# A selective-scan block with a feed-forward block: the input's row statistics formed one stage sooner

## The chip, the core and the metric

One core of one Trainium2 chip runs the kernel. The metric is device time in microseconds (us), the median over runs. The profile is of one execution on the same kind of core. Engines are called as in the profile: PE is TensorE (PEld its weight load), DVE is VectorE, ACT is ScalarE, POOL is GpSimd, and SP is SyncE, which issues every DMA of this kernel on one queue. The engines run side by side, and each works through its own instructions strictly in order.

## What is computed

The input `x` is 4 sequences of 2048 rows with 256 channels. A Mamba block and then a gated feed-forward block are added to it, each on rows that a layer norm has made ready:

```python
x = x + mamba(layernorm(x), ...)        # mamba adds its own input again
x = x + ffn(layernorm(x), ...)

# mamba
xn    = (x - mu) * rsqrt(var + 1e-5) * ln_w + ln_b
xi, z = split(xn @ W_in)                # 512 channels each
u     = silu(causal_conv4(xi) + conv_b)
dt_r, Bm, Cm = split(u @ W_xproj)       # 16, 64, 64
delta = softplus(dt_r @ W_dt + b_dt)
h_t   = h_(t-1) * exp(delta_t * A) + (delta_t * u_t) * B_t    # 512 channels x 64 states
y_t   = h_t . C_t
out   = x + ((y + u * D) * silu(z)) @ W_out
# ffn
out   = (silu(x @ wg.T) * (x @ wu.T)) @ wd.T                  # 768 hidden
```

The input of the Mamba block is a layer norm of a layer norm. The kernel forms both from one mean and one variance for each row.

## The kernel before

**Blocks and stages.** The 8192 rows are cut into 16 blocks of 512 rows (`NT` = 16, four for each sequence). The recurrence of a block is done in 16 groups of 16 pairs. A pair is a tile of 128 partitions (two channels times 64 states) by 512 time steps, and one `tensor_tensor_scan` on VectorE (line 1539) runs its whole recurrence. So a block needs 256 scans and the program 4096. A *stage* n, here and in the prediction, is the time of the 256 scans of block n. For each pair TensorE spreads delta over the states into a PSUM tile `a` (line 1528), ScalarE makes the decay factors with an exp in place (line 1534), and VectorE scans. There are four `a` tiles, so ScalarE can be at most four scans ahead. The other factor, delta times u times B, comes from a broadcast load of `dusc` into a tile `ring` (three of them, each one group) and is multiplied on GpSimd (line 1645). After its scan, TensorE contracts the ring with C (line 1563).

**Dense work.** While the scans of block n run, the other engines prepare block n+1 and finish block n-1. The function at line 1628, `dense`, takes these parts in order:

- `front(n+1)`: load x (`load_x`), row statistics (`layer_norm`), normalise into `xn`, store the residual to `rsum`, transpose to `xnT`
- `back(n-1)`: gate y, project out, add the residual, form sums for the second norm
- `front_a(n+1)`: project `xi` and convolve into `u`
- `front_b(n+1)`: project z (`project_z`), one silu over `u` and both z tiles (lines 997 to 1001: a table load, three activations, and a table load back to exp), then the dt projection, B and C, and four rounds of softplus
- `back_b(n-1)`: the feed-forward block, with a silu of its own (lines 1264 to 1267)

**How `layer_norm` works.** For the input (`sums` is None) VectorE runs four `bn_stats` on 128 x 256 each (line 491), then four `bn_aggr` (line 492) that write mean and variance into a PSUM bank `lp`. ScalarE then does five small steps on that (two of line 530, then 540, 541, 542: variance plus eps, log, exp, square), and VectorE does three small ones (545, 550, 555), one step of Newton's method and the bias. The results are two small tiles `rs` and `nm`.

**The planner.** The order of instructions on each engine isn't written by hand. Every operation is noted with an engine, a reckoned cost, what it reads and writes, and, for dense work, a due step. `dense` spreads due steps evenly over the stage by cumulated cost, from scan 8 to scan 244 (`D_SPAN`):

```python
tot = sum(o.cost for o in os)
t, lo, hi = 0.0, n * 256 + span[0], n * 256 + span[1]
for o in os:
    o.step = lo + (hi - lo) * t / tot if n >= 0 else -1000
    t += o.cost
```

`Planner.run` then places operations one by one. For each engine it takes the ready operation with the lowest score, which is its earliest start plus a bias. Work of the scan stream (kind S) has bias 0; dense work (kind D) has 17 ns for each step that it is ahead of its due step, kept between -230 and 170. So dense work that is late goes ahead of a scan that is ready at the same time, and dense work that is early goes behind it. ScalarE and TensorE add 300 ns to an operation that would hold up the stream. `after=` makes an operation ready when another one *starts*, without a data dependence.

**Buffers.** Named tiles rotate. `w4` has four (128 x 1024 floats); it carries `xt`, `xn`, `xnT`, the two z tiles `szs` (the gate buffers), and x1, xn, xT, hmb of `back_b`. Turns are taken strictly in program order, so a load into a `w4` tile can be issued only when all the turns before it have been taken and one tile is free. `ps` has four PSUM banks. Dense work takes banks in program order too, and only when two of them are free. `s4` has eight small tiles, `bst` four.

Of the kernel before, what the change touches and what calls it, by code (L numbers as in the profile page):

```python
# [20 lines left out]
P = 128  # L21
T = 512
DM = 256
DI = 512
# [314 lines left out]
def mamba_ffn_kernel(  # L339
# [5 lines left out]
    nc = tc.nc  # L345
# [30 lines left out]
    op, buf = pl.op, pl.buf  # L376
# [14 lines left out]
    win = const("win", [P, 2, 2 * DI])  # L391
# [38 lines left out]
    def tok(t):  # L430
        return t.t.rearrange("p a t -> p (a t)").rearrange("p (s c) -> p s c", s=4)
# [32 lines left out]
            one(s)  # L464
        return sums

    def layer_norm(src, blocks=range(4), twice=False, sums=None):

        nb = len(blocks)
        m = 2 if twice else 1
        lp = buf("ps")
        sq4 = buf("s4") if sums else None
        ve, rs, nm = buf("s4"), buf("s4"), buf("s4")

        def sq():
            return lp.t[:, 16 : 16 + m * nb]

        def col(b):  # L480
            return b.t[:, 0 : m * nb]

        def mv():
            return lp.t[:, 0 : 2 * nb].rearrange("p (s c) -> p s c", c=2)

        def two(v):
            return v.rearrange("p (m s) -> p m s", m=m)

        def stats(j, s):
            st = buf("bst")  # L490
            op("DVE", 326, lambda: nc.vector.bn_stats(st.t, tok(src)[:, s, :]), [(src, s // 2)], [st])
            op("DVE", 205, lambda: nc.vector.bn_aggr(mv()[:, j, :], st.t), [st], [(lp, 0, j)])

        def spread(s):
            op(
                "ACT", act(DM, ptr=1) + ACC,
                lambda: nc.scalar.activation(
                    lp.t[:, DM : 2 * DM], tok(src)[:, s, :], AF.Square,
                    bias=sums.t[:, 4 + s : 5 + s], accum_out=sq4.t[:, s : s + 1],
                ),  # L500
                [(src, s // 2), (sums, 4)], [(lp, 2), (sq4, s)],
            )

        if sums is None:
            for j, s in enumerate(blocks):
                stats(j, s)
            mk = [(lp, 0, j) for j in range(nb)]
        else:
            op(
                "ACT", 180,  # L510
                lambda: nc.scalar.activation(sums.t[:, 4:8], sums.t[:, 0:4], AF.Copy, scale=-1.0 / DM),
                [(sums, s) for s in range(4)], [(sums, 4)],
            )
            op(
                "ACT", 180, lambda: nc.scalar.copy(lp.t[:, 0:4], sums.t[:, 4:8]), [(sums, 4)], [(lp, 3)],
            )
            for s in range(4):
                spread(s)
            mk = [(sq4, s) for s in range(4)]

        def var_in():
            return mv()[:, :, 1] if sums is None else sq4.t[:, 0:4]

        def minus_mean():
            return mv()[:, None, :, 0] if sums is None else lp.t[:, None, 0:4]

        def var(i):
            op(
                "ACT", 180,
                lambda: nc.scalar.activation(  # L530
                    ve.t[:, i * nb : (i + 1) * nb], var_in(), AF.Copy,
                    bias=EPS * EPS if i else EPS, scale=(1.0 + EPS if i else 1.0) / (1 if sums is None else DM),
                ),
                mk, [(ve, i)],
            )

        for i in range(m):
            var(i)
        vk = [(ve, i) for i in range(m)]
        op("ACT", 180, lambda: nc.scalar.activation(col(rs), col(ve), AF.Ln), vk, [rs])  # L540
        op("ACT", 180, lambda: nc.scalar.activation(col(rs), col(rs), AF.Exp, scale=-0.5), [rs], [rs])
        op("ACT", 180, lambda: nc.scalar.activation(sq(), col(rs), AF.Square), [rs], [(lp, 1)])
        op(
            "DVE", TINY,
            lambda: nc.vector.scalar_tensor_tensor(sq(), sq(), -0.5, col(ve), ALU.mult, ALU.mult),
            [(lp, 1)] + vk, [(lp, 1)],
        )
        op(
            "DVE", TINY,
            lambda: nc.vector.scalar_tensor_tensor(col(rs), sq(), 1.5, col(rs), ALU.add, ALU.mult),  # L550
            [(lp, 1), rs], [rs],
        )
        op(
            "DVE", TINY,
            lambda: nc.vector.scalar_tensor_tensor(  # L555
                two(nm.t[:, 0 : m * nb]), minus_mean().to_broadcast([P, m, nb]), 1.0 if sums else -1.0,
                two(rs.t[:, 0 : m * nb]), ALU.mult, ALU.mult,
            ),
            (mk if sums is None else [(lp, 3)]) + [rs], [nm],
        )  # L560
        return rs, nm
# [197 lines left out]
    rest, gates, norms, last = {}, {}, {}, {}  # L759
# [12 lines left out]
    def front(n):  # L772
        r = n % R
        xt = load_x(n) if n else x0
        rs, nm = layer_norm(xt, twice=True)
        rp = buf("s4")
        op("ACT", 180, lambda: nc.scalar.activation(rp.t[:, 0:4], rs.t[:, 0:4], AF.Copy, bias=1.0), [rs], [rp])
        xn = buf("w4")
        normalise(xn, xt, (rs, nm), o=4)

        def keep():
            normalise(xt, xt, (rp, nm))
            store(rsum[r], lambda: tok(xt), 524288, halves(xt), [("rsum", r)])

        if n:
            keep()
        else:
            last["keep"] = keep
        xnT = buf("w4")

        def ev_t(c):
            def ev(ps):
                op(
                    "ACT", act(T, True, 2),
                    lambda: nc.scalar.activation(  # L795
                        xnT.t[:, c, :], ps.t, AF.Identity, bias=lnb[:, c : c + 1], scale=lnw[:, c : c + 1]
                    ),
                    [ps, "lnw", "lnb"], [(xnT, c)],
                )

            return ev

        for c in range(2):
            transposes(xn, c, ev_t(c))
        rest[n] = xnT
# [66 lines left out]
    def project_z(n):  # L872
        xnT = rest[n][0]
        szs = gates[n] = [buf("w4"), buf("w4")]

        def ev_z(k):
            def ev(ps):
                op(
                    "ACT", act(T, True), lambda: nc.scalar.copy(szs[k // 2].t[:, k % 2, :], ps.t),
                    [ps], [(szs[k // 2], k % 2)],  # L880
                )

            return ev

        for k in range(4):
            project(win, DI + k * P, xnT, ev_z(k), ["win"])

    def mix(n):
        r = n % R
# [98 lines left out]
    def front_b(n):  # L988
        b, q, r = n // NQ, n % NQ, n % R
        xnT, u = rest[n]  # L990
        uk = [(u, k) for k in range(4)]
        if n:
            project_z(n)
            szs = gates[n]
            zk = [(z, k) for z in szs for k in range(2)]

            def silu():
                nc.scalar.activation(u.t, u.t, AF.Silu)
                for h in range(2):
                    nc.scalar.activation(szs[h].t, szs[h].t, AF.Silu)  # L1000
                nc.scalar.preload_act_table_set(EXP_LN)

            o = op("ACT", 6400, silu, uk + zk, uk + zk)
            o.tail = -1283.0
            for k in uk:
                o.tails[k] = -3250.0
        else:

            def silu_a():
                nc.scalar.activation(u.t[:, 0:3, :], u.t[:, 0:3, :], AF.Silu)  # L1010

            def silu_b():
                nc.scalar.activation(u.t[:, 3, :], u.t[:, 3, :], AF.Silu)
                nc.scalar.preload_act_table_set(EXP_LN)

            op("ACT", 2900, silu_a, uk[0:3], uk[0:3])
            op("ACT", 1900, silu_b, uk[3:4], uk[3:4]).tail = -1283.0

        dtr = buf("xi")

        def mm_dt(k):
            return (
                430,
                lambda ps: nc.tensor.matmul(
                    ps[32 * k : 32 * k + 32, :], framed(wxp, k), u.t[:, k, :], start=True, stop=True
                ),
            )

        def ev_dt(ps):
            op(  # L1030
                "ACT", act(T, True, 1),
                lambda: nc.scalar.activation(dtr.t[:, 0:T], ps.t, AF.Identity, bias=dm[:, 2:3]), [ps, "dm"], [dtr],
            )

        last["dt"] = job([mm_dt(k) for k in range(4)], uk + ["wxp"], ev_dt)[-1:]

        rest[n] = (xnT, u, dtr)
        for m in range(2 if n == 0 else 0):
            softplus(n, m)
        mix(n)  # L1040
        for m in range(4 if n else 0):
            softplus(n, m)
        if n:
            gate(n)
# [673 lines left out]
```

## Time and profile before

| | |
|---|---|
| median of 3 runs | 4940.54 us (4936.31 to 4943.96) |
| profiled execution | 4944.55 us, of which the span of instructions is 4942.8 |
| granted TensorE clock | 0.976 |
| DMA | 1299.87 MB, mean 263 GB/s, 68.6% of the 16 engines' time in the queue of SP |
| `bn_stats` (L491) | 68 times, 409 ns median |
| `bn_aggr` (L492) | 68 times, 166 ns median |
| load of x (`w<-in`, 512 KB) | 15 times, 8.6 us median from issue to landing |
| reload of x1 (`w<-rsum`, 512 KB) | 31 times, 8.3 us median |
| silu of u and z (L998 to L1001) | 15 times, 6.4 us |
| stages 1 to 14, first scan to first scan | 299.5 to 307.5 us |

A line of the groups names source line, engine, operation, what it writes and reads, tile shapes and count; after the bar stand busy time in us and the mean of one in ns, then idle time of the engine just before these instructions and who ended it. A line of the timeline has start, length, engine, line, operation and count; a number in brackets is idle time of the engine before it.

### The profile page before, as it was taken

What the parts mean: (1) busy time and instruction counts of PE and PEld (TensorE: products, weight loads), DVE (VectorE), ACT (ScalarE), POOL (GpSimd) and SP (SyncE); (2) the same over time, 40 slices, a digit from 0 to 9 for tenths busy, and PEclk for the clock granted to TensorE, in tenths of its full rate; (3) what the DMA queues carried; (4) which work ended last, traced back from release to release, by engine and by line L of the source; (5) the groups of instructions that cost most, each with busy time, mean ns of one, the idle gap of its engine ahead of it and who ended that gap; (6) DMA issues with size and microseconds to landing.
All of it is one profiled execution on the core that took longest, in us unless ns stands there. A gap on an engine that the chain in (4) does not pass through costs nothing. (4 is left out here: it accounts for less than half of the span.)

```text
span 4942.8 us, 116006 instructions
## 1 busy us (share of the span) xinstructions
PE 4433.3 (90%) x46924; PEld 2205.2 (45%) x46924; DVE 4734.0 (96%) x4576; ACT 4005.2 (81%) x7378; POOL 4695.2 (95%) x862
## 2 busy tenths in 40 slices
PE   7889989998988999989999899989989999898888
PEld 3434444444444444444444444444444444444435
DVE  7999999999999999999999999999999999999996
ACT  6788878778788887888878788887878878888774
POOL 6999999999999999999999999999998999999994
PEclk9999999999999999999999999999999999999999
DMA  8676776667766777677667676677776767676762
GB/s 295 237 282 252 284 272 266 265 242 287 265 266 257 272 266 280 263 266 279 262 264 278 259 277 255 263 291 267 274 263 247 280 265 282 255 290 253 264 248 86
DMA packets 306347, 1299.87 MB, mean 263 GB/s; under 512 B 33617, under 2 KB 134737, under 8 KB 174866
## 3 DMA queue, kind: packets, MB, share of 16 engines
q1 hardware_dynamic: 305810, 1292.44, 68.6%
q8 instruction: 369, 6.05, 0.5%
q14 instruction: 168, 1.38, 0.1%
HBM read 1186.94 MB, written 105.38 MB: 261 GB/s over the span
## 5 line engine op out<-in xcount | busy, mean ns | idle before, releaser
L1539 DVE TENSOR_TENSOR_SCAN ring<-a,ring 128x512 f32<-128x512 f32 x4096 | 4594.2, 1198 | 103.7 <-ACT a L1534 81.2
L1645 POOL TENSOR_TENSOR ring<-ring,b 128x4088 f32<-128x4088 f32 (+2 forms) x512 | 4540.0, 8897 | 154.3 <-DMA ring<-dusc 116.9
L1534 ACT ACTIVATE a<-a,a 128x512 f32<-128x512 f32 x4096 | 2702.2, 666 | 677.2 <-PE a L1528 647.1
L1528 PE MATMUL a<-stk,selb 128*128 128x512 bf16 x5088 | 1809.3, 391 | 407.4 <-DVE ring L1539 374.7
L1563 PE MATMUL ps<-ring,cz 128*32 128x128 f32 x32768 | 1235.9, 280 | 19.4 <-issue 12.4
L1528 PEld LDWEIGHTS <-selb 128*128 128x128 bf16 x5088 | 471.2, 98 | 1347.6 <-issue 1274.2
L1563 PEld LDWEIGHTS ps<-ring,cz 128*32 128x32 f32 x32768 | 811.1, 110 | 541.4 <-issue 478.0
L596 PE MATMUL ps<-w,wgu 128*128 128x512 f32 x720 | 373.5, 600 | 0.0
L1584 ACT COPY mm<-ps 128x512 f32<-128x512 f32 x512 | 304.5, 596 | 37.2 <-PE ps L1563 36.3
L1597 PE MATMUL ps<-mm,exs 128*32 128x128 f32 (+1 forms) x4112 | 285.3, 407 | 1.3 <-ACT mm L1584 1.0
L596 PE MATMUL ps<-w,win 128*128 128x512 f32 x512 | 260.7, 594 | 0.3 <-ACT w L795 0.3
L830 PE MATMUL ps<-xi,w 128*128 128x512 f32 x480 | 245.8, 593 | 0.0
L1597 PEld LDWEIGHTS ps<-mm,exs 128*32 128x32 f32 x4112 | 116.8, 118 | 202.8 <-ACT a L1534 81.6
L1148 PE MATMUL ps<-wd,w 128*128 128x256 f32 x720 | 195.8, 386 | 0.0
L596 PEld LDWEIGHTS ps<-w,wgu 128*128 128x128 f32 x720 | 138.1, 192 | 111.2 <-issue 58.5
L1148 PEld LDWEIGHTS ps<-wd,w 128*128 128x128 f32 x720 | 132.4, 189 | 42.1 <-issue 14.7
L949 PE MATMUL ps<-w,ident 128*128 128x512 f32 x248 | 133.3, 620 | 6.7 <-ACT ps L944 5.9
L596 PEld LDWEIGHTS ps<-w,win 128*128 128x128 f32 x512 | 96.8, 190 | 89.7 <-issue 57.5
L1148 PE MATMUL ps<-wout,w 128*128 128x256 f32 x480 | 128.4, 388 | 0.9
L830 PEld LDWEIGHTS ps<-xi,w 128*128 128x128 f32 x480 | 88.9, 188 | 82.6 <-issue 62.2
L571 ACT ACTIVATE w<-w,s,s 128x256 f32<-128x256 f32 x192 | 112.8, 597 | 0.9 <-DVE s L555 0.9
L1255 POOL TENSOR_TENSOR w<-w,w 128x512 f32<-128x512 f32 x90 | 113.4, 1281 | 0.0
(154 smaller groups left out, 2416.9 us busy)
## 6 DMA issues: line engine op xcount, KB each, us to landing
ring<-dusc SPq DMA_DIRECT2D x1023, 1024.0 KB, 7.9
stk<-dsc SPq DMA_DIRECT2D x256, 96.0 KB, 5.9
qd<-w SPq DMA_DIRECT2D x32, 512.0 KB, 9.5
szd<-w SPq DMA_DIRECT2D x32, 512.0 KB, 11.6
dusc<-w SPq DMA_DIRECT2D x63, 256.0 KB, 6.4
dsc<-pk SPq DMA_DIRECT2D x63, 256.0 KB, 6.5
rsum<-w SPq DMA_DIRECT2D x31, 512.0 KB, 6.8
w<-rsum SPq DMA_DIRECT2D x31, 512.0 KB, 8.3
```

Of the source, the lines that this page charges most:

```text
L596: lambda ps: nc.tensor.matmul(ps, w[:, c, o : o + P], xT.t[:, c, :], start=(c == 0), stop=(c == 1)),
L830: lambda: nc.tensor.matmul(ps.t, dg.t[:, j * P : (j + 1) * P], xi.t[:, j : j + T], start=(j == 0), stop=(j == 3)),
L949: lambda: nc.tensor.matmul(ps.t, m, t.t, start=False, stop=True, skip_group_check=True),
L1148: lambda ps: nc.tensor.matmul(ps[:, (s % 2) * DM : (s % 2 + 1) * DM], src(k)[:, s * P : (s + 1) * P], w[:, k, :], start=False, stop=(k == ...
L1255: "POOL", 1230, lambda: nc.gpsimd.tensor_tensor(hm(k), hm(k), up.t, ALU.mult),
L1528: "PE", 216, lambda: nc.tensor.matmul(a.t, selb[:, p, :], stk.t, start=True, stop=True),
L1534: lambda: nc.scalar.activation(a.t, a.t, AF.Exp, scale=a2f[:, idx : idx + 1]), [a, "a2"], [a],
L1539: nc.vector.tensor_tensor_scan(v, a.t, v, 0.0, ALU.mult, ALU.add)
L1563: nc.tensor.matmul(pm.t[cg * 32 : cg * 32 + 32, (r8 % 4) * P : (r8 % 4 + 1) * P], framed(cz, blk), ring.t[:, :, blk * 8 : blk * 8 + 8], st ...
L1584: nc.scalar.copy(mm.t[:, hb * 4 : hb * 4 + 4].rearrange("p r a t -> p (r a t)"), pm.t)
L1597: nc.tensor.matmul(ex.t[jh * 32 : jh * 32 + 32, a * 16 : b * 16], framed(exs, jh * 2 + jl), mm.t[:, a:b, :, jh * 2 + jl], start=(jl == 0), ...
L1645: e.tensor_tensor(v, v, b2.t[:, None, t0:].to_broadcast([P, m, T - t0]), ALU.mult)
```

## The change

After the last z projection of block m, `front_b(m)` now also loads the x of block m+1 and runs its whole `layer_norm`, and keeps `rs` and `nm` in `norms`. The `bn_stats` carry `after=`: they may start once the last z matmul has started. `front(m+1)`, a stage later, loads x once more and takes the kept statistics; if there are none (block 0 and block 1) it forms them as before. So the statistics of blocks 2 to 15 move, and 14 loads of 512 KB are added. In program order the new `w4` turn lies between the gate buffers and the x1 of `back_b`, and the new `ps` turn between the last bank of z and the bank of the dt projection.

```diff
-    def layer_norm(src, blocks=range(4), twice=False, sums=None):
+    def layer_norm(src, blocks=range(4), twice=False, sums=None, after=()):
...
         def stats(j, s):
             st = buf("bst")
-            op("DVE", 326, lambda: nc.vector.bn_stats(st.t, tok(src)[:, s, :]), [(src, s // 2)], [st])
+            op("DVE", 326, lambda: nc.vector.bn_stats(st.t, tok(src)[:, s, :]), [(src, s // 2)], [st], after=after)
             op("DVE", 205, lambda: nc.vector.bn_aggr(mv()[:, j, :], st.t), [st], [(lp, 0, j)])
...
     def front(n):
         r = n % R
         xt = load_x(n) if n else x0
-        rs, nm = layer_norm(xt, twice=True)
+        rs, nm = norms.pop(("in", n), None) or layer_norm(xt, twice=True)
...
         for k in range(4):
-            project(win, DI + k * P, xnT, ev_z(k), ["win"])
+            last["z"] = project(win, DI + k * P, xnT, ev_z(k), ["win"])[-1]
...
         if n:
             project_z(n)
+            if n + 1 < NT:
+                xt = load_x(n + 1)
+                norms["in", n + 1] = layer_norm(xt, twice=True, after=[last["z"]])
             szs = gates[n]
```

## The prediction

> **What bounds the kernel now.** First the busy table and the groups. VectorE is busy 4734.0 us of a 4942.8 us span, most of it in 4096 scans:
>
> ```profile
> PE 4433.3 (90%) x46924; PEld 2205.2 (45%) x46924; DVE 4734.0 (96%) x4576; ACT 4005.2 (81%) x7378; POOL 4695.2 (95%) x862
> ...
> L1539 DVE TENSOR_TENSOR_SCAN ring<-a,ring 128x512 f32<-128x512 f32 x4096 | 4594.2, 1198 | 103.7 <-ACT a L1534 81.2
> ```
>
> The scans are the clock of the program. Back to back, one starts 1.115 us after the other (median of 3777 neighbours; 1198 ns is the record, whose ends overlap). So only VectorE's idle time, 209 us, and its other work can be won. The view of waits says what the scans lack:
>
> ```profile
> DVE ring L1539 <- ACT a L1534: 81.2, 43, 4.9
> ```
>
> 43 times they wait for the exp on ScalarE, 4.9 us at the longest. The timeline of VectorE, then ScalarE, around the silu of u and z in stage 7 shows one of these:
>
> ```profile
> 2304.97 6.77 DVE L1539 TENSOR_TENSOR_SCAN ring<-a,ring 128x512 f32<-128x512 f32 x6
> 2315.98 4.57 DVE L1539 TENSOR_TENSOR_SCAN ring<-a,ring 128x512 f32<-128x512 f32 x4 [4.24 <-ACT a L1534]
> ```
> ```profile
> 2308.87 1.28 ACT L998 ACT_TABLE_LOAD   x1
> 2310.16 1.91 ACT L998 ACTIVATE w<-w 128x2048 f32<-128x2048 f32 x1
> 2311.98 1.99 ACT L1000 ACTIVATE w<-w 128x1024 f32<-128x1024 f32 x2
> 2313.99 1.28 ACT L1001 ACT_TABLE_LOAD   x1
> 2315.28 2.40 ACT L1534 ACTIVATE a<-a,a 128x512 f32<-128x512 f32 x4
> ```
>
> ScalarE is away for 6.4 us; the four `a` buffers carry the scans 2.9 us into it, then VectorE idles 4.24 us. This hole (4.0 to 4.9 us in stages 1 to 14, 2.8 in stage 0) is the one the change aims at. But there is a second one, at the silu of the feed-forward part. Stage 6, VectorE:
>
> ```profile
> 2109.28 5.65 DVE L1539 TENSOR_TENSOR_SCAN ring<-a,ring 128x512 f32<-128x512 f32 x5
> 2114.85 0.47 DVE L1458 TENSOR_TENSOR ps<-ps,a 128x128 f32<-128x128 f32 x2
> 2115.23 1.39 DVE L491 BATCH_NORM_STATS2 bst<-w 128x6 f32<-128x256 f32 x4
> 2116.57 0.07 DVE L820 MEMSET xi<- 128x3 f32 x2
> 2117.78 4.57 DVE L1539 TENSOR_TENSOR_SCAN ring<-a,ring 128x512 f32<-128x512 f32 x4 [1.14 <-ACT a L1534]
> ```
>
> The statistics of the next block's input already lie in it, at all 13 feed-forward silus that have a next block. Only the aggregates and the last three small steps stand between scans, at the start of a stage:
>
> ```profile
> 2194.72 0.16 DVE L492 BATCH_NORM_AGGREGATE ps<-bst 128x2 f32<-128x6 f32 x1
> 2194.79 1.19 DVE L1539 TENSOR_TENSOR_SCAN ring<-a,ring 128x512 f32<-128x512 f32 x1
> 2195.89 0.16 DVE L492 BATCH_NORM_AGGREGATE ps<-bst 128x2 f32<-128x6 f32 x1
> 2195.97 1.19 DVE L1539 TENSOR_TENSOR_SCAN ring<-a,ring 128x512 f32<-128x512 f32 x1
> 2197.07 0.39 DVE L492 BATCH_NORM_AGGREGATE ps<-bst 128x2 f32<-128x6 f32 x2
> 2197.37 2.32 DVE L1539 TENSOR_TENSOR_SCAN ring<-a,ring 128x512 f32<-128x512 f32 x2
> 2199.61 0.15 DVE L545 SCALAR_TENSOR_TENSOR ps<-ps,s 128x8 f32<-128x8 f32 x1
> 2199.66 1.21 DVE L1539 TENSOR_TENSOR_SCAN ring<-a,ring 128x512 f32<-128x512 f32 x1
> ```
>
> **The change, part by part.** It moves the statistics of blocks 2 to 15 (14 moves) and adds 14 loads of 512 KB.
>
> 1. The four `bn_stats` (1.33 us by their starts) leave the feed-forward hole. That hole's end is set by ScalarE's table load and exp, so nothing is won: its idle time grows from some 1.4 to 2.7 us. In their new place they use 1.33 of 4.24 us: also nothing. If that cover is missed they cost 1.33 x 13 = 17.3 us.
>
> 2. Aggregates and small steps leave a full stretch. Scan starts 1.18 us apart with one aggregate between them, against 1.115, price it: 0.066 us each for two, 0.288 for the pair (median of 14), 0.056, 0.0715 and 0.0705 for L545, L550, L555; together 0.62 us. Won if all hide: 14 x 0.62 = 8.7 us. Their records alone say 4 x 0.171 + 0.155 + 2 x 0.14 = 1.12 us, or 15.7 us, the far end of the gain; I take 0.62, since the scans' starts are what counts.
> The Trainium skill (VectorE: DVE Perf Modes, the section on the TRN2 errata) holds that every small operation pays a fixed term, measured at about 150 cycles of 0.96 GHz. As an estimate from that page, seven such terms are 1.09 us, and 14 blocks would give 15.3 us in place of 8.7; the scans' starts above speak against it.
>
> 3. The small ScalarE steps (two L530, L540, L541, L542) take 0.87 us at the start of stage 7 (2197.49 to 2198.36 us). Now they come due as the silu ends, where VectorE waits for the first exp. Ahead of it they lengthen the hole by 0.87; behind it they cost nothing: 0 to 14 x 0.87 = 12.2 us. I take half, 6.1.
>
> 4. Place in VectorE's queue. The planner prefers an operation that is past its due step. Adding the kernel's own costs, 78,534 of 205,815 precede the new load in a stage, so it is due at step 8 + 236 x 0.38 = 98; the silus come at scan 109 to 116 of their stage. So the statistics are late and pass any scan that is ready, once their data and the last z matmul (some 2 to 3 us before the silu) allow. In 5 of the 13 stages the second gate buffer is taken 11 us before the silu, so x is there early and the statistics (2.1 us) push the last scans into the silu. These fill only what the four buffers hold, so between 0 and one scan of 1.115 us is lost. I take 0.5: 2.5 us.
>
> 5. In the other 8 stages the gate buffer is taken 3.3 to 3.5 us before the silu, and x can only be issued then. The nearest row is `w<-rsum`, also 512 KB, issued at that very place (it takes the next turn of the same buffers): in the six stages with a record it landed 2.0 to 5.6 us after the silu's start. Statistics then end at 4.1 to 7.7, the next scan wants VectorE at 7.1: loss 0 to 0.6, I take 0.2 x 8 = 1.6 us. The slowest ring load there took 13.95 us: issued 2.9 before the silu it would land at 11.1, and cost 6 us. Behind the waiting `bn_stats` stand all later scans.
>
> 6. DMA and queues. 512 KB at the mean 263 GB/s is 2.0 us, after 0.6 us of issue on SP, ahead of ring loads. GpSimd waits for these 116.9 us in all, but its products are ready 7 to 12 us before their scans in this part of a stage: nothing. Without that lead, 14 x 2 = 28 us. The reload of x1 in `back_b`, one turn later, slips by some 2 us; its first reader comes 11 us after the silu's start.
>
> 7. The aggregates hold a PSUM bank through the silu, and the dt projection takes its bank after them, so it may start 3 to 5 us later. The stores that hang on it go out up to scan 159 (first half) and are read from scan 237 on: nothing; the cover is some 75 scans. The next stage's normalisation, whose statistics now exist, starts a few us sooner; it is not on the path either.
>
> Sum: -8.7 + 6.1 + 2.5 + 1.6 = +1.5 us on the profiled execution's 4944.55, so 4946. That execution lies 4.0 above the median of 4940.54: **4942 us**, no change that counts. A measurement of this kernel tells about 0.2% (10 us) from no change. Around this stands the re-planning of the whole order: the stages 1 to 14 take 299.5 to 307.5 us from first scan to first scan for nearly equal work, so a shift of 1 us in each, 14 us in all, is easy either way. That makes the forecast's own range 4930 to 4954.
>
> **Rivals.**
> - *Faster, 4925:* everything hides behind the exps and frees its whole record, 15.7 us, or the new order loses less elsewhere. For it: the hole has 4.24 us for 2.1 us of work. Against: scan starts show 0.62, and the costliest part was hidden before.
> - *Slower by queue order, 4960:* point 4 holds in every stage. The statistics go ahead of the scans before the silu, a whole scan is lost to the four buffers, and the ScalarE chain stands ahead of the exps: 14 x (1.115 + 0.87) - 8.7 = +19. It decides once more than some 9 of 14 silus do so. For it: the due steps. Against: 8 stages get x too late for that.
> - *Slower by a late x, 4965:* `bn_stats` placed on an arrival that comes 2 us late in each: 14 x 2 - 8.7 + 6.1 = +25. For it: two of the 13 waited for `w<-in` already, 0.13 and 0.56 us, with 5.3 us of lead. Against: the `w<-rsum` landings.
>
> **How the numbers follow.** Forecast 0.42, faster 0.22, queue order 0.26, late x 0.10. So faster 0.22, same 0.42, slower 0.36. The likeliest case gives 4942; the range, 4921 to 4970, takes in the three rivals.
>
> **What would show it.** Right: `bn_stats` near L998, that hole at 2 to 3 us, the feed-forward hole grown to 2.5 to 3, no aggregates at a stage's start, stage lengths unmoved. Queue order: `bn_stats` with starts before L998's table load, and L530 between L1001 and the first exp. Late x: waits of L491 for `w<-in` of over 1 us. The forecast is wrong if stages change by more than 0.7 us each, wherever that comes from.

## The result, and the profile after

The changed kernel takes 5017.07 us, median of 4 runs (5006.78 to 5024.72), against 4938.43 us of the kernel before, timed beside it (4 runs, 4931.7 to 4943.96). The ratio is 1.0155 with a 95% interval of 1.0142 to 1.0168: 78.6 us slower (78 us in what follows), and outside the predicted range. The profiled execution has a span of 5014.4 us at a granted clock of 0.969 (before 4942.8 us at 0.976), 71.6 us more.

The busy table, the group of the scans and two waits of the changed kernel (in a wait: engine, tile and line that waited, who ended it, sum in us, times, longest; lines behind the edit stand three lower down, so 1542 is the scan, 1537 its exp and 1648 GpSimd's product):

```profile
PE 4405.9 (88%) x46629; PEld 2224.0 (44%) x46920; DVE 4736.4 (94%) x4576; ACT 4006.8 (80%) x7378; POOL 4696.0 (94%) x862
...
L1542 DVE TENSOR_TENSOR_SCAN ring<-a,ring 128x512 f32<-128x512 f32 x4096 | 4597.7, 1199 | 158.4 <-ACT a L1537 126.8
```
```profile
DVE ring L1542 <- ACT a L1537: 126.8, 78, 6.6
...
ACT w L942 <- DMA dusc<-w: 82.1, 21, 7.1
```

VectorE is busy for as long as before (4736.4 against 4734.0 us). What grew is its idle time. The scans waited 43 times for an exp, 81.2 us in all; now 78 times, 126.8 us. And ScalarE, which makes the exps, waits in line 942 for a *store*, `dusc<-w`, 82.1 us in all. The same line stood in the view of waits before:

```profile
ACT w L942 <- DMA dusc<-w: 15.4, 11, 3.6
```

Sorting VectorE's idle time over 50 ns by where it stands, from both traces, gives where the 71.6 us went (2.4 of them are busy time, 69 idle time):

| idle time of VectorE, us | before | after |
|---|---|---|
| at the silu of u and z | 62.8 | 42.6 |
| at the silu of the feed-forward part | 23.3 | 40.5 |
| scans waiting for an exp elsewhere | 16.3 | 79.1 |
| scans elsewhere, waiting for nothing that the profile shows | 1.5 | 19.6 |
| scans elsewhere, waiting for GpSimd | 0.3 | 3.3 |
| other instructions of VectorE elsewhere | 99.6 | 87.7 |

The first row is the gain that the change can aim at (after it, 26.8 of the 42.6 us stand ahead of a moved small step, line 545, and not ahead of a scan), and the second is the price of it that step 1 gives. The third, 62.8 us more, is what the prediction has no term for. Of the 102 us in rows three to five after the change, 90.3 stand in, or less than 12 us behind, a wait of ScalarE for one of two stores, `dusc<-w` (line 942) or `dsc<-pk` (line 956); before, 8.5 of 18.1 did.

One such place, in stage 9, where the scans stand still for 6.64 us. The timeline of the changed kernel, VectorE first, then ScalarE, then SP:

```profile
2990.22 0.66 DVE L957 TENSOR_TENSOR w<-ps,w 128x512 f32<-128x512 f32 x1
2990.80 4.55 DVE L1542 TENSOR_TENSOR_SCAN ring<-a,ring 128x512 f32<-128x512 f32 x4
3002.00 2.34 DVE L1542 TENSOR_TENSOR_SCAN ring<-a,ring 128x512 f32<-128x512 f32 x2 [6.64 <-ACT a L1537]
```
```profile
2992.38 0.28 ACT L962 COPY x<-w 128x64 f32<-128x64 f32 x1
2992.51 0.70 ACT L1537 ACTIVATE a<-a,a 128x512 f32<-128x512 f32 x1
2993.09 0.63 ACT L974 CAST pk<-ps 128x512 bf16<-128x512 f32 x1
3000.78 0.63 ACT L942 ACTIVATE w<-w 128x512 f32<-128x512 f32 x1 [7.06 <-DMA dusc<-w]
3001.32 0.64 ACT L1537 ACTIVATE a<-a,a 128x512 f32<-128x512 f32 x1
```
```profile
2984.28 2.53 SPq L425 DMA_DIRECT2D ring<-dusc  x4
2990.91 0.33 SPq L428 DMA_DIRECT2D dusc<-w  x1
```

A round of softplus makes delta times u in a tile `w` (line 957) and stores it to `dusc`. The next round takes a `w2` tile for a temporary (`rl`, line 942), and it is the very tile that the store is still reading. Line 942 stands in ScalarE's order, so the exps behind it wait too: the four `a` tiles carry the scans for another 2 us or so, then VectorE stands. The store lands 9.8 us after its issue, at 3000.7 us. Four ring loads of 1 MB each went out on the same queue between 2984.28 and 2986.81 us, ahead of the store; the last of them landed at 3000.05 us. The windows of the changed kernel show them (length in us, busy time and count of PE, PEld, DVE, ACT, POOL, then the granted clock, the DMA engines' share and GB/s):

```profile
2986.00:2988.00 2.00, 2.00 (x14) 0.75 (x15) 2.00 (x3) 1.80 (x5) 2.00 (x1) 1.00 0.90 381
...
2996.00:2998.00 2.00, 0.00 (x0) 0.00 (x0) 0.00 (x0) 0.00 (x0) 2.00 (x1) 1.00 0.97 348
2998.00:3000.00 2.00, 0.00 (x0) 0.00 (x0) 0.00 (x0) 0.00 (x0) 2.00 (x1) 0.76 0.32 116
```

The DMA engines are full (0.90 to 1.05 in all windows from 2986 on) up to 2998 us, and the store lands when they have run empty. In the last two windows everything but GpSimd stands still for it.
The Trainium skill (DMA: Bandwidth & Descriptors, the section on queues, rings and completion order) says that each DMA engine consumes its descriptors in ring order. A store issued after 4 MB of loads on one queue is then moved after them, and these windows agree.

**Why that tile.** The planner gives a tile back when the operation that was *placed last* among its users ends. The store is placed first; after it comes the copy of line 962, a short operation of ScalarE that saves the block's first column and reads the same tile. In the plan this store ends at 171.53 us of its stage, the copy earlier, and line 942 is put into the tile at 167.48. Counted in the plan, a tile is taken ahead of the end of its store at 11 places before the change (seven of them by under 1 us) and at 25 after it (six of them by these 4.05 us, at most by 4.6 us). The places where line 942 waits longest in the trace are among them. The generated program still waits for the landing, so nothing is overwritten; the wait is only one that the plan doesn't know of. Its own total went *down* with the change, from 4892 to 4885 us.

### The profile page after: what moved, and what is told of

Its sections match the earlier page's. It is cut to its first block, busy times and chain, and to the rows that moved or that the text cites. A ratio compares the mean times of both kernels' runs of the same rounds, so it can differ in the third digit from the quotient of the medians.

```text
span 5014.4 us, 115723 instructions
## 1 busy us (share of the span) xinstructions
PE 4405.9 (88%) x46629; PEld 2224.0 (44%) x46920; DVE 4736.4 (94%) x4576; ACT 4006.8 (80%) x7378; POOL 4696.0 (94%) x862
## 5 line engine op out<-in xcount | busy, mean ns | idle before, releaser
L1542 DVE TENSOR_TENSOR_SCAN ring<-a,ring 128x512 f32<-128x512 f32 x4096 | 4597.7, 1199 | 158.4 <-ACT a L1537 126.8
L1531 PE MATMUL a<-stk,selb 128*128 128x512 bf16 x4806 | 1755.5, 394 | 417.5 <-DVE ring L1542 381.8
```

Of the source, the lines that this page charges most:

```text
L1531: "PE", 216, lambda: nc.tensor.matmul(a.t, selb[:, p, :], stk.t, start=True, stop=True),
L1542: nc.vector.tensor_tensor_scan(v, a.t, v, 0.0, ALU.mult, ALU.add)
```

## The experiments

**Theory A:** the 78 us are these waits for stores, in one particular order of instructions; moving the statistics isn't what costs. **Rival B:** the statistics ahead of the scans at the silu, with ScalarE's small chain ahead of the exps, cost it. **Rival C:** the second load of x, or any new order of that length, costs it. A kernel's ratio is to the kernel before, run beside it, whose median was 4936 to 4942 us throughout.

**1. The same order with more tiles.** Each of the four `w2` tiles becomes two that alternate. The planner still counts four, so every engine's order of instructions is that of the changed kernel, and a round that takes a tile finds in it the one that was left a turn earlier. To make room, the up projection of the feed-forward part uses the gate's weights, and two of the six slices of the down projection's weights are used twice. Instructions and transfers are the same in number and size, but the result is not that of the block: a kernel to measure with, not to use.

```diff
-        "w2": tiles("w2", 4, [P, T]),
+        "w2": tiles("w2", 8, [P, T]),
...
-                b.t = self.phys[b.tag][b.slot]
+                i, half = b.slot, self.twin.get(b.tag)
+                if half:
+                    turn = self.used[b.tag, i] = self.used.get((b.tag, i), 0) + 1
+                    i += half * (turn % 2)
+                b.t = self.phys[b.tag][i]
```

> The changed kernel in the same order of instructions, with eight w2 tiles used in turn where the planner still reckons with four, so that a softplus round no longer writes into a tile whose store has not landed. To make room the up projection of the feed-forward part uses the gate's weights and the down projection reuses two of six slices of its weights; instructions and transfers are the same in number and size. Theory (stores): the loss is ScalarE waiting at L942 for the dusc store, which starves the scans; its 82 us of waits fall below 10 us, and the time falls by 50 to 80 us, to 4937 to 4967. Rival (traffic or queue place): the second load of x, or the statistics' place in VectorE's queue, cost the time; it stays above 5000.

4916.15 us, ratio 0.9957 (0.9942 to 0.9972): 101 us less than the changed kernel, and 21 below the range that theory A had. The group of line 942, which stands at line 948 here, in the changed kernel and then in this one:

```profile
L942 ACT ACTIVATE w<-w 128x512 f32<-128x512 f32 x62 | 39.2, 632 | 83.9 <-DMA dusc<-w 82.1 <-PE ps L949 1.5
```
```profile
L948 ACT ACTIVATE w<-w 128x512 f32<-128x512 f32 x62 | 39.8, 642 | 0.0
```

The same stretch of stage 9, on VectorE, has no idle time left:

```profile
2924.70 13.46 DVE L1548 TENSOR_TENSOR_SCAN ring<-a,ring 128x512 f32<-128x512 f32 x12
2938.07 0.67 DVE L963 TENSOR_TENSOR w<-ps,w 128x512 f32<-128x512 f32 x1
2938.66 13.47 DVE L1548 TENSOR_TENSOR_SCAN ring<-a,ring 128x512 f32<-128x512 f32 x12
```

The store is as slow as it was (median from issue to landing 7.2 us, in the changed kernel 7.3). It is just no longer waited for. That more is won than the 82.1 us of waits fits the places in the changed kernel: after a wait of 6.42 us in stage 1, the scans stand 5.33 us, and another 0.37 and 1.15 us before ScalarE is ahead again. The waits for the other store, `dsc<-pk`, remain (22.3 us).

**2. The control:** the kernel before with the same eight tiles.

> The kernel before with the same eight w2 tiles in its own unchanged order, and the same reuse of feed-forward weights. Control for the run above. Theory (stores): L942 waits only 15 us here, of which some reach the scans, so 4925 to 4938, a gain of at most 15 us. Rival (more tiles are worth as much to any order): a gain of 50 us or more here too.

4930.54 us, 0.9985 (0.9975 to 0.9994): about 6 us. So the tiles, and the weights thinned out to make room for them, are worth 6 us where few such waits exist, and 101 where many do. With eight tiles, the change is 14 us *faster*. That is theory A, and B and C can't explain it: statistics, loads and order are those of the changed kernel.

**3 and 4. The planner corrected**, with and without the change: a tile comes free at the latest end among its users, a store's landing included.

```diff
             b.left -= 1
+            if end > b.over[0]:
+                b.over = (end, o.eng)
             if not b.left:
-                self.free[b.tag].append((end, o.eng, b.slot))
+                self.free[b.tag].append((*b.over, b.slot))
```

> The changed kernel with one repair in the planner: a tile comes free when the latest of its users ends, a store's landing included, and not when the user that was placed last ends. So rounds of softplus are ordered behind the reckoned landing of the store. Theory (stores): the places where a tile is taken before its store has landed fall from 25 to none in the plan; stores still land later than reckoned, so part of the waits stays: 4930 to 4975. Rival (any other cause): within 15 us of the changed kernel's 5017.

> The kernel before with the same repair of the planner. Theory (stores): there are 11 such places before, most under 1 us, so little to win, and the order is re-planned: 4925 to 4960. Rival (the repair itself is worth much in any order): 4900 or less.

With the change 4898.55 us (4897.73 to 4899.75), 0.9922 (0.9908 to 0.9937), the fastest of all kernels here, 119 us below the changed one and below the expected range too. Without it 4936.97 us, 1.0000 (0.9991 to 1.0009). The correction alone does nothing for the kernel before, whose early takes were few and mostly short; with it the change is worth 38 us. The waits of the corrected kernel with the change (scan 1545, exp 1540, and 945 for 942):

```profile
DVE ring L1545 <- ACT a L1540: 62.7, 37, 4.2
...
ACT w L945 <- DMA dusc<-w: 11.7, 6, 3.8
```

**5 and 6. Statistics behind the scans**, a test of rival B. Due steps of the moved statistics are put off by 40 scans, first with the planner as it was, then corrected:

```diff
+                a = len(pl.ops)
                 norms["in", n + 1] = layer_norm(xt, twice=True, after=[last["z"]])
+                later.update(pl.ops[a:])
...
+        for o in os:
+            if o in later:
+                o.step += 40
```

> The changed kernel, planner unrepaired, with the due step of the moved statistics raised by 40 (their load and all twelve other steps of that layer_norm). They then stand behind ready scans and behind ready exps at the silu, so the last scan before the hole is not pushed out and the small ScalarE steps do not delay the first exp. The new order happens to take no tile before its store has landed. Theory (stores cost the time, the queue order at the silu some): the large waits of L942 go, 4880 to 4920. Rival (the moved statistics cost the time in any order): above 4990.

> The changed kernel with the repaired planner (4898.6 us), and the due step of the moved statistics raised by 40. Theory: at most one scan (1.115 us) and 0.87 us of small ScalarE steps are won back at each of 14 silus, so up to 28 us: 4870 to 4892. Rival (place in the queue at the silu is worth nothing): 4895 to 4902.

Uncorrected 4945.24 us, 1.0010 (0.9999 to 1.0021). Taken alone it looks as if rival B were right, since 72 us are gone; but this order also has few early takes of a tile: 8 in its plan, and not none, as the expectation has it. Its waits for stores are 25 us, against 109 in the changed kernel, so it can't tell A from B; and the time met neither range. The corrected pair can. Locally the late place does what it should. VectorE at the silu of u and z in stage 6, in the changed kernel:

```profile
2033.83 0.73 DVE L491 BATCH_NORM_STATS2 bst<-w 128x6 f32<-128x256 f32 x2
...
2035.72 2.31 DVE L1542 TENSOR_TENSOR_SCAN ring<-a,ring 128x512 f32<-128x512 f32 x2
2040.61 0.17 DVE L545 SCALAR_TENSOR_TENSOR ps<-ps,s 128x8 f32<-128x8 f32 x1 [2.58 <-ACT ps L542]
2040.82 0.17 DVE L550 SCALAR_TENSOR_TENSOR s<-ps,s 128x8 f32<-128x8 f32 x1
2041.19 1.22 DVE L1542 TENSOR_TENSOR_SCAN ring<-a,ring 128x512 f32<-128x512 f32 x1 [0.20 <-ACT a L1537]
```

The silu's table load starts at 2033.06 there. The statistics go ahead of the last two scans, and after the hole come two small steps ahead of the first one. In the corrected kernel with late statistics:

```profile
1973.33 7.89 DVE L1548 TENSOR_TENSOR_SCAN ring<-a,ring 128x512 f32<-128x512 f32 x7
...
1982.73 0.40 DVE L495 BATCH_NORM_AGGREGATE ps<-bst 128x2 f32<-128x6 f32 x2
1985.42 5.68 DVE L1548 TENSOR_TENSOR_SCAN ring<-a,ring 128x512 f32<-128x512 f32 x5 [2.30 <-ACT a L1543]
```

All scans first, then the statistics in the hole, 2.30 us of it left, and the scans go on with the first exp. So it is in every stage. Yet that kernel takes 4926.82 us, 0.9971 (0.9957 to 0.9984), 28 us *more* than the corrected one without the delay. The expectation of 4870 to 4892 us was a miss. The idle time at the silu fell by 6.4 us, but the rest of the stage is planned anew, and there it grew by more: instructions other than scans waited 85.3 us, against 69.8, and scans away from both silus 27.1, against 11.1. Rival B is out as the cause of the 78 us (in experiment 1 the order at the silu is that of the changed kernel, and the time is gone), and the local price of a bad place at the silu is smaller than the noise of re-planning.

**7 and 8. The parts of the change**, each on the corrected planner: only the second load of x, whose data nobody reads; then the load and the `bn_stats`, while the aggregates and all that follows them stay in the next stage.

```diff
             project_z(n)
+            if n + 1 < NT:
+                load_x(n + 1)
```
```diff
+                norms["in", n + 1] = row_stats(xt, after=[last["z"]])
...
-        rs, nm = layer_norm(xt, twice=True)
+        rs, nm = layer_norm(xt, twice=True, sts=norms.pop(("in", n), None))
```

> The kernel before with the repaired planner (4937.0 us) and only the second load of x at the new place; nothing reads it, and the statistics stay at the start of the next stage. Theory (traffic is nothing, but a w4 turn and the due steps shift): 4930 to 4960. Rival (the second load costs the time by itself): 4975 or more.

> The repaired planner, second load of x, and only the four bn_stats moved to the new place; aggregates, the small ScalarE steps and the last VectorE steps stay at the start of the next stage. Theory A (the gain of 38 us with the repaired planner comes from the next stage starting its normalisation at once): no gain here, 4925 to 4950. Theory B (it comes from filling the hole at the silu): most of the gain here too, 4900 to 4915.

The load alone: 4968.36 us, 1.0054 (1.0037 to 1.0070), 31 us more than the corrected kernel before, though nobody waits for its data and its waits for stores are 9 us. That lies above the expected range and below the rival's. The turn that it takes of a `w4` tile shifts the dense work: the last store of a softplus round goes out at scan 183 in place of 174, the feed-forward silu begins at 206 in place of 195 (medians of the stages). That this order costs the 31 us, and not the traffic, is argued: the corrected kernel with the whole change has the same 14 loads and is 70 us faster. With the `bn_stats`: 4925.61 us, 0.9972 (0.9961 to 0.9984), 43 less; and the rest of the change takes off another 27 to 4898.55. Theory B (most of the gain by the `bn_stats` alone) is out; the time is at the lower end of theory A's range, with 11 us of gain left where it has none. So rival C has a true part, since the load costs, but the sum of the parts is a gain of 38 us. That an addition of work takes 43 us *off* says again how much of these numbers is the new order and not the work itself.

**9 to 13. Another order, by a nudge.** Dense work is spread from scan 10 instead of 8 (`D_SPAN`), in the kernel before, the changed one, the corrected changed one, the corrected one before, and the changed one with eight tiles.

```diff
-D_SPAN = (8, 244)
+D_SPAN = (10, 244)
```

> The kernel before with the same nudge; 15 such places. Theory: 4940 to 4985, slower than before by re-planning alone, with somewhat more waiting for stores than the 27 us of before. Rival (a new order costs nothing): 4930 to 4945.

> The changed kernel, planner unrepaired, with one number of the plan nudged that has nothing to do with the statistics: dense work of a stage starts to fall due at scan 10 instead of 8. Asks whether the 78 us belong to this one order. The new order takes a tile before its store has landed in 19 places (25 in the changed kernel, 11 before). Theory (the loss goes with these places): 4960 to 5010, with L942 and L956 waiting 40 to 90 us for stores. Rival (the moved statistics as such): 5010 to 5025. Rival (pure chance of the order): anything, without relation to these waits.

> The changed kernel with the repaired planner (4898.6 us) and the same nudge. Theory: with the repair the moved statistics stay worth something against before under another order too: 4895 to 4930. Rival (4898.6 was the luck of one order): 4935 or more.

> The kernel before with the repaired planner and dense work due from scan 10. Partner of the changed kernel with both (4941.5 us). Theory (with the repair the change is worth something under any order, since the dense chain starts some 30 scans sooner): 4955 to 4985. Rival (4898.6 was the luck of one order, and the change is worth nothing): 4935 to 4948.

> The order of the changed kernel due from scan 10, planner unrepaired (4986.7 us), unchanged, with eight w2 tiles in turn and the feed-forward weights reused as before (up projection with the gate's weights, two of six slices of the down projection's weights used twice). Theory (waits for stores cost the time in this order too): its 49 us of waits at L942 go and the time falls by 30 to 60 us, to 4927 to 4957. Rival (other waits of this order): 4970 or more.

| span from scan 10 | time, us | ratio (95%) |
|---|---|---|
| before | 4985.18 | 1.0089 (1.0074 to 1.0104) |
| changed | 4986.69 | 1.0089 (1.0070 to 1.0109) |
| corrected, before | 4955.87 | 1.0037 (1.0024 to 1.0049) |
| corrected, changed | 4941.53 | 1.0007 (0.9997 to 1.0016) |
| changed, eight tiles | 4944.47 | 1.0011 (1.0002 to 1.0020) |

Two scans' difference in the due steps cost the kernel *before* some 43 us (4941.78 us beside it). From there, the change costs nothing: 4985 and 4987. Eight tiles take 42 us off the changed one, again with the same order. Of the five expectations four were met, the kernel before at the edge of its range. The corrected changed kernel missed its own (4895 to 4930) and lies in that of the rival, the luck of one order; against its partner the change still gains 14 us. So the 78 us isn't a property of the change. It is that of two plans that were drawn, one with few early takes of a tile, one with many.

**14 and 15. A third order**, from scan 6, both corrected.

> The kernel before with the repaired planner and dense work due from scan 6. Partner of the run below. Re-planning alone: 4925 to 4965.

> The changed kernel with the repaired planner and dense work due from scan 6. Theory: 15 to 45 us below its partner. Rival: within 10 us of it, or above.

4923.42 us, 0.9967 (0.9954 to 0.9980), without the change, just below the expected range, and 4914.10, 0.9952 (0.9935 to 0.9968), with it: 9 us, where 15 to 45 had been expected and the rival had at most 10. On the corrected planner the change gains 38, 9 and 14 us at spans from 8, 6 and 10. So more than half of the 38 seems to belong to that one order.

**16. More slack for a store:** the corrected planner keeps a tile for 3 us beyond the store's reckoned landing.

> The changed kernel with the repaired planner, and 3 us added to the landing of every transfer when the planner decides when its tile is free again. Theory: the 15 us that L942 and L956 (their lines shift) still wait for stores fall below 5, of which VectorE feels a part: 4890 to 4900, the fastest order. Rival (a new order costs more than these waits): 4905 to 4930.

4901.19 us, 0.9920 (0.9905 to 0.9935), the same as without the slack, though the wait of that line falls from 11.7 to 0.5 us; neither range was met. The waits that the correction leaves are hidden by the four `a` tiles in part: three of the six reached the scans, for 5.5 us, and that is less than what a new order shifts.

## Why the prediction was wrong

**Step 1** (`bn_stats` leave the feed-forward hole) was right as to the mechanism. VectorE in the changed kernel at the feed-forward silu of stage 6, whose hole was 1.14 us:

```profile
2140.26 3.43 DVE L1542 TENSOR_TENSOR_SCAN ring<-a,ring 128x512 f32<-128x512 f32 x3
2143.60 0.47 DVE L1461 TENSOR_TENSOR ps<-ps,a 128x128 f32<-128x128 f32 x2
2144.07 0.07 DVE L820 MEMSET xi<- 128x3 f32 x2
2146.83 3.45 DVE L1542 TENSOR_TENSOR_SCAN ring<-a,ring 128x512 f32<-128x512 f32 x3 [2.70 <-issue]
```

All these holes together grew by 17.2 us, the 1.33 x 13 = 17.3 of that step. The work has gone and the scans come no sooner.

**Step 2** (8.7 us from small steps that leave a full stretch) can't be read from the time by itself; the aggregates are gone from the stage's start, as it says. At the silu they and the first two small steps lie in the hole, and what comes behind it holds the next eight scans up by 0.1 to 0.2 us in most stages. So most of the 8.7 us was probably won.

**Step 3** (ScalarE's small chain ahead of the first exp, in half the silus) was a little low: it is so in 10 of 14, and there the first exp starts 7.5 instead of 6.6 us after the silu does. The scans resume 8.1 us after it, 7.1 to 7.3 before and in the other four. That is some 10 x 0.87 = 8.7 us for the 6.1 of the sum. ScalarE at the silu of stage 6 in the changed kernel:

```profile
2038.18 1.28 ACT L1004 ACT_TABLE_LOAD   x1
...
2039.64 0.25 ACT L530 ACTIVATE s<-ps 128x4 f32<-128x4 f32 x2
...
2040.51 2.38 ACT L1537 ACTIVATE a<-a,a 128x512 f32<-128x512 f32 x4
```

**Step 4** was right on the order, wrong on how often, and wrong on the price: the statistics, past due, go ahead of ready scans in all 14 stages, where I had 5, but no scan is lost by it. In the changed kernel's stage 14, which has no statistics, the last two scans before the hole start 0.77 and 1.89 us after the silu's table load does; with the statistics ahead of them, in stage 1, at 2.03 and 3.54. They are the same scans, later, in time that the hole would have idled, and the next one comes when its exp does: 7.28 us after the table load in stage 14 and in stages 0, 3, 7 and 11, where only the statistics are in the way. So the 2.5 us of this step weren't paid. The rival *queue order* has both its orders right, in 14 and in 10 of 14 silus, and its point of decision, 9 of 14, is met (though its sign, `bn_stats` before the table load, is not: they start 0.8 us or more after it). But of its price, 14 x (1.115 + 0.87), only the 8.7 us of step 3 was paid. The idle time at this silu *fell* by 20.2 us, since the statistics now lie in it, and the 62.8 us more of waiting for exps stand elsewhere in the stage.

**Step 5** was wrong: no silu after stage 0 waits for x. The planner gave the gate buffer earlier: in the eleven stages with a record x is issued 6 to 10 us ahead of the silu and lands within 0.5 us of its start. `bn_stats` waited for a load once, 1.6 us. The rival *late x* never occurred.

**Step 6** gave the DMAs and queues nothing. By itself the second load does cost: 31 us in experiment 7, most likely by the turn of a buffer and the order that follows from it, not by the transfer, which nobody waited for.

**Step 7 is the step that failed.** It says of the softplus stores that they "go out up to scan 159 (first half) and are read from scan 237 on: nothing; the cover is some 75 scans". That is right of the data in `dusc`, and it is the wrong reader. A store also holds the tile it comes *from*, and the next round of softplus wants that tile a few us later. This cover was never priced, and the row that shows it stood in the waits before: line 942, waiting for `dusc<-w`, 15.4 us in 11 places, up to 3.6 us, beside line 956 for `dsc<-pk`, 11.2 us. Experiment 1 shows that it is the cause: one more turn of tiles, the order kept, and 101 us go. That the early takes went from 11 to 25 with the change is how this plan was drawn: with dense work due from scan 10, the changed kernel takes no longer than the one before.

The same step has the next stage's normalisation "a few us sooner; it is not on the path". Its result `xnT` is ready at about scan 253 of the stage ahead (median) instead of scan 28 to 31 of its own, some 30 scans or 33 us sooner. With the planner corrected, the change gains 38 us: between the two corrected kernels VectorE's idle time falls by 19.2 us at the silu and by 21.7 in instructions other than scans, and grows by 15.6 at the feed-forward silu. Of the second, 6.3 us can be tied to the earlier front: line 1119, the gate of `back`, waits 16.0 us for TensorE without the change, 9.7 with it (the same line is 1122 there), and still 16.0 in experiment 8, whose front stands at scan 24 to 30 as before. Most of the rest is at the softplus product (line 960, 17.7 to 6.8 us), and which part of the change it comes from is open.

**The re-planning** was put at 14 us either way, from the spread of stage lengths. By the nudges it is 14 to 43: the corrected kernel before went from 4936.97 to 4923.42 and 4955.87 us, the kernel before from 4942 to 4985. It also moved things that I took as fixed: the silu came at scan 100 to 104 of its stage, not 109 to 116, and the first store of a softplus round at 129 in ten stages. Stages 1 to 14, 299.5 to 307.5 us each before, run from 298.5 to 314.5; two of the three that prepare the first block of a sequence, where the copies of line 962 don't exist, are among the three shortest, 299.4 and 298.5 us. This fits the planner's fault, since without the copy the tile is not given back before its store ends.

What stays open: waits for stores and time are not in proportion over all kernels (43 us of waits at 4985.18 in the nudged kernel before, 36 at 4941.53 in the nudged corrected one, 9 at 4968.36 with the load alone). Beside the stores, a plan loses time by its order in ways that no run here took apart.

## What to carry to other kernels

A store has two readers to be late for: whoever loads the data, and whoever next takes the tile that it leaves from; price both, above all where the taker sits in the in-order queue of the engine that feeds the critical one, and read every wait of that engine for a store, however small its sum, as a sign of what a new order can make of it. Where a planner sets the order, a change of work is also a new draw: measure it with the same nudge on both kernels, or with the order held, before the difference is put down to the work. And see when the planner thinks a buffer free: one line that used the latest end instead of the last one placed turned a loss of 78 us into a gain of 38 against the kernel before, in one order; 9 and 14 in two others.

## What the runs showed of the hardware

A 256 KB store on a queue shared with the loads lands 6.4 us (median, before) to 7.3 us (after) from its issue, and 9.8 us behind four loads of 1 MB. With the load alone, where the last stores of a stage go out nine scans later, it was 2.2 us, and that kernel was still slower than the one before. With eight tiles it was 7.2 us, and line 942 never waited. So the landing time of a store tells little by itself; whether its tile is wanted does.
